# Layer 3's query-key and score products on 12-bit halves, in three passes

## The chip, the cores and the metric

The kernel runs on one core of one Trainium2 chip. The metric is the device time of one execution in microseconds. The kernel before has a median of 963.69 us over 3 runs (963.59 to 963.74). The profiled execution, from which all other times here are read, spans 961.7 us.

## The reference, cut to what matters

`x` is 32 graphs of 512 nodes with 128 features, `adj` one 512 x 512 matrix. Four layers follow each other, each of the form `x = x + layer(relu(layernorm(x)), adj)`. The change concerns the last one:

```python
def _L3_gnn_ref(x, A_shape, q, k, v):
    Q = x @ q
    K = x @ k
    A = jnp.einsum('bnd,bmd->bnm', Q, K)
    A = A / jnp.sqrt(jnp.float32(input_dimension))
    A = jnp.tanh(A / 8.0) * 8.0
    A = jnp.exp(A) * A_shape
    A = A / jnp.sum(A, axis=-1, keepdims=True)
    out = A @ x @ v
    return out
...
h = jnp.maximum(_layernorm(x, axis=-1), 0.0)
x = x + _L3_gnn_ref(h, adj, L3_gnn_q, L3_gnn_k, L3_gnn_v)
```

All of it is in 32-bit floating point.

## The kernel before, in words

A tile is 128 partitions by a free dimension. The 32 graphs are taken in 16 pairs, `q` = 0 to 15, with `b` = 0 or 1 inside a pair. `x` stays in SBUF from the first layer to the last. Layer 0 is recorded in an order written out by hand; from layer 1 on, each pair of a layer is a Python generator (`layer1(r)`, `layer2(q)`, `layer3(q)`), and the loop at the end of the kernel steps all active generators in turn and lets one new one in per turn. The Tile framework's scheduler then sets the order on each engine within the data dependences. Each engine works its own queue off in order.

One pair of layer 3 goes through these stages. `normed` makes `h` on ScalarE, `transposed` turns it to `hT` (features on partitions) with 32 x 32 transposes on VectorE (L283) and two trips through DRAM. Then for each `b`:

- **qkh** (L1097): one matmul of the constant `qk` = q k^T with `hT`, 128 x 512, into one PSUM bank; VectorE copies it to SBUF as `qkh` in another column order (L1100).
- **hv** (L435, called from L1102): `hT` times `vw`, four 128 x 128 matmuls; VectorE copies the result beside a column of ones (L1105).
- **scores** (L1110): four matmuls, each of a 128-column block of `hT` (stationary) with all of `qkh` (moving), 128 x 512, one PSUM bank each; ScalarE takes tanh out of PSUM (L1111), then exp in place (L1113); VectorE and GpSimd multiply by the transposed adjacency `adjTx` (L1115; odd blocks on GpSimd).
- **av** (L1125): 16 matmuls of 128 x 129 that weigh `hv` with `ex`; VectorE divides by the row sum and adds to `x` (L1127, L1130), and the result leaves by DMA (L1135).

The yields in `layer3` decide what stands between two stages of the same pair. In the middle of layer 3 the order on TensorE is, in every turn: av of one pair's second graph, scores of the next pair's second graph, av and then qkh and hv of younger pairs, scores of a younger pair's first graph, qkh and hv of the youngest.

All PSUM work shares 8 banks. In the program a 32-bit matmul is one instruction; the profile shows it as two MATMUL records, each with its own weight load (LDWEIGHTS).

Of the kernel before, what the change touches and what calls it, by code (L numbers as in the profile page):

```python
# [8 lines left out]

F32 = mybir.dt.float32  # L10
F16 = mybir.dt.float16
BF16 = mybir.dt.bfloat16
AF = mybir.ActivationFunctionType
OP = mybir.AluOpType
AX = mybir.AxisListType

P = 128
QR = 32
NQR = P // QR
NEG = 9000000000000000.0  # L20
EPS = 1e-5


@with_exitstack
def kernel(
# [37 lines left out]
    nc = tc.nc  # L63
    B, N, D = x.shape
# [5 lines left out]
    const = ctx.enter_context(tc.tile_pool(name="const", bufs=1))  # L70
# [3 lines left out]
    work = ctx.enter_context(tc.tile_pool(name="work", bufs=4))  # L74
    bounce = ctx.enter_context(tc.tile_pool(name="bounce", bufs=4, space=bass.MemoryType.DRAM))

    def bank(name):
        return psum.tile([P, 512], F32, tag="bank", name=name)

# [7 lines left out]
    def square_tile(name):  # L87
        return const.tile([P, NT, N], F32, tag="square", name=name, bufs=4)

    def crossed(ap):  # L90

        return ap.rearrange("p (a b c) -> p b a c", a=NT, b=NQR)

    def split(ap):
        return ap.rearrange("p (a b c) -> p a b c", a=NT, b=NQR)
# [13 lines left out]
    def x_tile(pool, bufs):  # L109

        x = pool.tile([P, 2, 2, NT, D], F32, tag="x", name=f"x_{len(xq)}", bufs=bufs)
        xq.append(x)
# [8 lines left out]
    def load_rows(ap, name):  # L121
        o = ap.shape[0] // P
        w = const.tile([P, o, ap.shape[1]], F32, name=name)
        nc.sync.dma_start(w, ap.rearrange("(o f) g -> f o g", f=P))
        return w

    def load_bcast(ap, name):
        w = const.tile([P, D], F32, name=name)
        nc.sync.dma_start(w, bass.AP(tensor=ap.tensor, offset=ap.offset, ap=[[0, P], [1, D]]))
        return w  # L130
# [7 lines left out]
    kw = load_rows(k_w, "kw")[:, 0, :]  # L138
    ecol = const.tile([P, NK], F32, name="ecol")
    nc.sync.dma_start(ecol, e_l0.rearrange("o (k p) -> p (o k)", p=P))  # L140
# [27 lines left out]
    by_source.__enter__()  # L168
    cols = prep.tile([P, N], F16, name="cols")
    nc.gpsimd.iota(cols, pattern=[[1, N]], base=0, channel_multiplier=0,  # L170
# [6 lines left out]
    eps = const.tile([P, 1], F32, name="eps")  # L177
    nc.vector.memset(eps, EPS)
    nc.scalar.activation(prep.tile([P, 1], F32, name="powers"), eps, AF.Exp)
# [4 lines left out]

    known = prep.tile([P, NT, 2], F16, name="known")
    nc.vector.tensor_copy(known[:, :, 1], rows)
    upto = prep.tile([P, NT, N], F16, name="upto")
    for t in range(NT):
# [3 lines left out]
    shift, scale = {}, {}  # L192
# [5 lines left out]
    def early_stats(q, whole):  # L198
# [7 lines left out]
        for b in range(2):  # L206
# [7 lines left out]
            half = slice(0 if whole else 2 * b, 2 * b + 2)  # L214
            nc.gpsimd.tensor_scalar(sd[:, half], st[:, half, :, 2], 1.0 / D, EPS, OP.mult, OP.add)
            nc.gpsimd.tensor_scalar(sh[:, half], st[:, half, :, 1], -1.0, None, OP.mult)
# [41 lines left out]
    def feature_major(name):  # L258
        return work.tile([P, NQR, 2, P], F32, tag="hT", name=name, bufs=4)
# [39 lines left out]
    sums = {}  # L299
# [65 lines left out]
    def products(name, form, left, right, evict, order=ORDER, on=lambda k, p: p):  # L365


        banks = {}
        for k, g, first in order:
            if first:  # L370
                banks[g] = bank(f"p_{name}_{g}")
            form(on(k, banks[g]), left[k], right[k], first)
            evict(k, banks[g])
            yield
# [18 lines left out]
    def mixed(name, left, right, dst):  # L393

        m1 = dst[:, 0, H:], dst[:, 1, :H], dst[:, 1, H:]

        def evict(k, p):
            p = p[:, :H]
            if k == 1:
                nc.scalar.copy(m1[0], p)  # L400
            elif k == 6:
                nc.vector.tensor_add(m1[1], p, m1[0])
            elif k == 7:
                nc.vector.tensor_add(m1[2], p, m1[0])
            elif k == 5:
                return
            elif k == 2:
                nc.scalar.copy(dst[:, 0, :H], p)
            elif k == 4:
                nc.vector.tensor_add(dst[:, 0, H:], p, m1[0])  # L410
            elif k == 3:
                nc.vector.tensor_add(dst[:, 1, :H], p, m1[1])

        def evict2(k, p):
            evict(k, p)
            if k == 5:
                held.append(p)
            if k == 7:
                nc.vector.tensor_add(dst[:, 1, H:], held[0][:, :H], m1[2])

        held = []
        return products(name, by_feature, left, right, evict2)

    def at(hT, b):
        return lambda t: hT[:, t, b, :]
# [75 lines left out]

    m = prep.tile([P, NT, N], F16, name="m")
    rc = prep.tile([P, NT], F32, name="rc")
    att = square_tile("att")
    ident16 = prep.tile([P, P], F16, name="ident16")
    nc.gpsimd.tensor_copy(ident16, ident)
    keep_busy(12)
    for t in range(NT):
        nc.vector.tensor_scalar(m[:, t, :], adj_s[:, t, :], 0.0, None, OP.is_gt, OP.add,
                                accum_out=rc[:, t : t + 1])  # L510
        nc.gpsimd.tensor_scalar(att[:, t, :], m[:, t, :], -1.0, -NEG, OP.add, OP.mult)
    rch = prep.tile([P, NT], F16, name="rch")
    nc.vector.tensor_copy(rch, rc)

    pi = bank("p_incl")
    for t in range(NT):
        for s in range(t + 1):
            nc.tensor.matmul(pi[:, t : t + 1], upto[:, s, blk(t)], rch[:, s : s + 1],
                             start=(s == 0), stop=(s == t))
# [12 lines left out]
    qk = const.tile([P, D], F32, name="qk")  # L532
# [16 lines left out]
    parts = []  # L549
    for i in range(3):  # L550
        eh = prep.tile([P, NK], BF16, name=f"eh_{i}")
        nc.gpsimd.tensor_copy(eh, ecoln)
        part = prep.tile([P, NK], F32, name=f"part_{i}")
# [5 lines left out]
    hT = {q: feature_major(f"hT0_{q}") for q in range(4)}  # L559
# [5 lines left out]
    for t in range(NT):  # L565
# [4 lines left out]
        for j in range(NT):  # L570
            nc.tensor.matmul(pg[j // 2][:, j % 2, :], m[:, t, blk(j)], of_row[:, t, :],
                             start=(t == 0 and j % 2 == 0), stop=(t == NT - 1), skip_group_check=True)
    pb = bank("p_known")[:, : 2 * NK].rearrange("p (k e) -> p k e", e=2)
    for kk in range(NK):
        for t in range(NT):
            nc.tensor.matmul(pb[:, kk, :], of_row[:, t, blk(kk)], known[:, t, :],
                             start=(t == 0), stop=(t == NT - 1))
# [17 lines left out]
    for kk in range(NK):  # L595
        for j in range(NT):
            nc.tensor.matmul(pw[kk][:, j * P :], pgs[:, j, blk(kk)], upto[:, j, j * P :],
                             start=(j == 0), stop=(j == NT - 1), skip_group_check=True)
# [100 lines left out]
    late = ctx.enter_context(tc.tile_pool(name="late", bufs=4))  # L699
# [341 lines left out]
        yield  # L1041
        ln_stats(NQ - 1)

    msgs, values = [], {}

    def values_tile(q, b):

# [41 lines left out]
    def layer3(q):  # L1089
        h = normed(q)  # L1090
        yield
        hT = transposed(h, f"hT3_{q}")
        yield
        yield
        for b in range(2):
            pp = bank(f"p_qkh_{q}_{b}")
            nc.tensor.matmul(pp, qk, hT[:, :, b, :], start=True, stop=True)  # L1097
            both = values_tile(q, b)
            qkh = both[:, :N]
            nc.vector.tensor_copy(crossed(qkh), split(pp))  # L1100

            pv = projected(f"p_hv_{q}_{b}", (at(hT, b), vw))  # L1102
            hv = both[:, N : N + NT * (D + 1)].rearrange("p (t f) -> p t f", f=D + 1)
            nc.vector.memset(hv[:, :, D : D + 1], 1.0)
            nc.vector.tensor_copy(hv[:, :, :D], pv)  # L1105
            yield
            ex = square_tile(f"ex_{q}_{b}")
            for t in range(NT):
                ps = bank(f"p_score_{q}_{b}_{t}")
                nc.tensor.matmul(ps, hT[:, t, b, :], qkh, start=True, stop=True)  # L1110
                nc.scalar.activation(ex[:, t, :], ps, AF.Tanh, scale=1.0 / (8.0 * math.sqrt(D)))  # L1111
            for t in range(NT):
                nc.scalar.activation(ex[:, t, :], ex[:, t, :], AF.Exp, scale=8.0)  # L1113
                eng = nc.gpsimd if t % 2 and q + b > 0 else nc.vector
                eng.tensor_mul(split(ex[:, t, :]), split(ex[:, t, :]), crossed(adjTx[0][:, t, :]))  # L1115
            yield
            out_r = out[2 * q + b].rearrange("(t p) f -> p t f", p=P)
            rsum = stats.tile([P, NT], F32, tag="rsum", name=f"rsum_{q}_{b}", bufs=4)
            final = b == 1 and q == NQ - 1
            n = 1 if final else 2  # L1120
            for i0 in range(0, NT, n):
                po = bank(f"p_av_{q}_{b}_{i0}").rearrange("p (i f) -> p i f", i=2)[:, :n]
                for i in range(n):
                    for t in range(NT):
                        nc.tensor.matmul(po[:, i, : D + 1], ex[:, t, blk(i0 + i)], hv[:, t, :],  # L1125
                                         start=(t == 0), stop=(t == NT - 1))
                nc.vector.reciprocal(rsum[:, i0 : i0 + n], po[:, :, D])  # L1127
                for i in range(n):
                    xi = xt[q][:, b, i0 + i, :]
                    nc.vector.scalar_tensor_tensor(xi, po[:, i, :D], rsum[:, i0 + i : i0 + i + 1], xi,  # L1130
                                                   OP.mult, OP.add)
                if final:
                    nc.sync.dma_start(out_r[:, i0, :], xt[q][:, b, i0, :])
            if not final:
                nc.sync.dma_start(out_r, xt[q][:, b])  # L1135
# [69 lines left out]
```

## Time and profile before

| | busy us | share of the span |
|---|---|---|
| TensorE matmuls (PE) | 953.3 | 99% |
| TensorE weight loads (PEld, overlap the matmuls) | 780.8 | 81% |
| VectorE (DVE) | 584.4 | 61% |
| ScalarE (ACT) | 469.1 | 49% |
| GpSimd (POOL) | 423.8 | 44% |

| group of layer 3 | records | busy us |
|---|---|---|
| p_av L1125, matmuls | 1024 | 119.9 |
| p_score L1110, matmuls | 256 | 115.2 |
| p_hv L435, matmuls | 256 | 33.7 |
| p_qkh L1097, matmuls | 64 | 32.7 |
| exp L1113, ScalarE | 128 | 76.7 |
| tanh L1111, ScalarE | 128 | 71.9 |
| mask L1115, GpSimd | 62 | 80.3 |
| mask L1115, VectorE | 66 | 46.1 |

A group's line gives the busy time of all its records together and the mean length of one. Matmul records overlap: [...]the mean length of one (593 ns for p_score) is more than the distance between two starts. What a matmul costs a busy TensorE is that distance, and the view of the chain of work that ended last, in order of time, gives it, since there each step counts only from the end of the step before. An average over the whole span says little here: the four layers have different loads, and the change touches only the last 300 us or so.

### The profile page before, as it was taken

To read this page: it belongs to the slowest core of one execution; us is meant where nothing else is said; L and a number is where in the kernel's file an instruction comes from. 1 tells how busy PE (TensorE), PEld (TensorE's weight loads), DVE (VectorE), ACT (ScalarE), POOL (GpSimd) and SP (SyncE) were. 2 spreads that over 40 slices of the span, in tenths; PEclk is the share of its full clock that TensorE was granted. 3 is DMA by queue.
4 is the path that set the end of the run, shared out by engine and by line. 5 is a ranking of instruction groups with operands and counts; after the bars stand their busy time and mean duration, and the time that the engine had idled before them with its cause. 6 is when DMAs were issued, how large, how long until landed. Compare 5 with 4: busy or idle time off the path is not lost.

```text
span 961.7 us, 15152 instructions
## 1 busy us (share of the span) xinstructions
PE 953.3 (99%) x5465; PEld 780.8 (81%) x5465; DVE 584.4 (61%) x1326; ACT 469.1 (49%) x1054; POOL 423.8 (44%) x470
## 2 busy tenths in 40 slices
PE   8999999999999999999999999999999999999998
PEld 4899999898989999899877777777677777767776
DVE  8888885846536545656667665665654444444444
ACT  5865542442232233277627655444765445544553
POOL 5878987833517522513333444433032233223322
PEclk9999999999999999999999999999999999999999
DMA  9356532441341230343333433223121121211111
GB/s 252 62 166 185 160 108 84 104 110 55 102 136 45 66 88 23 110 110 96 89 99 97 126 91 85 74 82 88 56 88 56 55 77 44 72 61 45 55 33 44
DMA packets 83913, 86.04 MB, mean 89 GB/s; under 512 B 6784, under 2 KB 74624, under 8 KB 83840
## 3 DMA queue, kind: packets, MB, share of 16 engines
q1 hardware_dynamic: 83552, 84.57, 31.6%
q8 instruction: 43, 0.70, 0.3%
q10 hardware_dynamic: 288, 0.52, 0.2%
q14 instruction: 30, 0.25, 0.1%
HBM read 44.17 MB, written 40.89 MB: 88 GB/s over the span
## 4 chain that ended last, share of the span: by engine, by line
PE 96%; ACT 2%; DVE 1%; DMA 0%; POOL 0%; issue 0%; DVEq 0%; ACTq 0%
PE p_av L1125 12%; PE p_score L1110 11%; PE p_l_c L386 8%; PE p_w L435 6%; PE p_l_d L386 6%; PE p_msgT_c L379 5%; PE p_l_a L386 4%; PE p_x1T_c L379 4%; PE p_l L435 3%; PE p_feat L435 3%; PE p_hv L435 3%; PE p_qkh L1097 3%; PE p_x1T_a L379 3%; PE p_msgT_d L379 3%; PE p_g L435 3%; PE p_x1T_d L379 3%
## 5 line engine op out<-in xcount | busy, mean ns | idle before, releaser
L247 ACT ACTIVATE h<-x,sh,rs 128x128 f32<-128x128 f32 x512 | 209.2, 484 | 51.7 <-PE p_x1T_d L379 21.7
L1115 POOL TENSOR_TENSOR ex<-ex,adjTx 128x512 f32<-128x512 f32 x62 | 80.3, 1295 | 208.3 <-ACT ex L1113 202.8
L1111 ACT ACTIVATE ex<-p_score 128x512 f32<-128x512 f32 x128 | 71.9, 587 | 122.8 <-issue 113.0
L1125 PEld LDWEIGHTS p_av<-qkh_hv,ex 128*128 128x128 f32 x1024 | 118.4, 191 | 8.4 <-issue 7.4
L1125 PE MATMUL p_av<-qkh_hv,ex 128*128 128x129 f32 x1024 | 119.9, 274 | 0.0
L1110 PE MATMUL p_score<-qkh_hv,hT 128*128 128x512 f32 x256 | 115.2, 593 | 0.0
L283 DVE STREAM_TRANSPOSE hb_hT<-h 128x512 f32<-128x512 f32 x120 | 82.0, 698 | 23.7 <-ACT h L247 22.6
L1115 DVE TENSOR_TENSOR ex<-ex,adjTx 128x512 f32<-128x512 f32 x66 | 46.1, 703 | 82.0 <-ACT ex L1113 81.9
L227 DVE BATCH_NORM_STATS2 bn<-x 128x6 f32<-128x256 f32 x248 | 89.8, 419 | 0.6
L1110 PEld LDWEIGHTS p_score<-qkh_hv,hT 128*128 128x128 f32 x256 | 46.2, 190 | 46.5 <-issue 44.5
L1113 ACT ACTIVATE ex<-ex 128x512 f32<-128x512 f32 x128 | 76.7, 630 | 1.9
L356 POOL TENSOR_TENSOR rt_feat<-feat,feat 128x256 f32<-128x256 f32 x16 | 11.6, 725 | 136.4 <-ACT feat L1064 136.4
L958 ACT COPY w<-p_w 128x512 f32<-128x512 f32 x32 | 18.2, 574 | 106.1 <-PE p_w L435 106.1
L356 POOL TENSOR_TENSOR rt_w<-w,rt_w 128x512 f32<-128x512 f32 x16 | 20.4, 1273 | 110.3 <-DVE rt_w L356 92.0
L435 PE MATMUL p_w<-th,x1T 128*128 128x128 f32 x256 | 49.5, 275 | 0.0
L435 PE MATMUL p_w<-th,hs 128*128 128x128 f32 x256 | 49.5, 275 | 0.0
L435 PEld LDWEIGHTS p_hv<-vw,hT 128*128 128x128 f32 x256 | 33.6, 192 | 15.3 <-issue 8.1
L1075 POOL TENSOR_TENSOR x<-x,phi2b 128x256 f32<-128x256 f32 x64 | 44.5, 727 | 0.0
L435 PEld LDWEIGHTS p_w<-th,hs 128*128 128x128 f32 x256 | 39.9, 192 | 0.7
L1064 ACT ACTIVATE feat<-feat 128x512 f32<-128x512 f32 x32 | 20.1, 629 | 41.4 <-DVE feat L1063 41.4
L1130 DVE SCALAR_TENSOR_TENSOR x<-p_av,rsum,x 128x128 f32<-128x128 f32 x128 | 39.1, 347 | 1.9
L712 POOL TENSOR_TENSOR hd<-hT,adiag 128x512 f32<-128x512 f32 x32 | 39.6, 1274 | 0.2 <-ACT adiag L838 0.2
(238 smaller groups left out, 2039.7 us busy)
## 6 DMA issues: line engine op xcount, KB each, us to landing
d_hT<-hb_hT SPq DMA_DIRECT2D x240, 128.0 KB
hT<-d_hT SPq DMA_DIRECT2D x60, 512.0 KB
x<-in_x_dram SPq DMA_DIRECT2D x32, 256.0 KB
out_dram<-x SPq DMA_DIRECT2D x31, 256.0 KB
adjT_d<-adj_squares SPq DMA_DIRECT2D x4, 256.0 KB
sq<-in_adj_dram SPq DMA_DIRECT2D x4, 256.0 KB
adjTx<-adjT_d SPq DMA_DIRECT2D x4, 256.0 KB
adj_s<-in_adj_dram ACTq DMA_DIRECT2D x2, 256.0 KB
```

Of the source, the lines that this page charges most:

```text
L227: nc.vector.bn_stats(st[:, k].rearrange("p e s -> p (e s)"), xt[q][:, b, t : t + 2, :].rearrange("p t f -> p f t"))
L247: nc.scalar.activation(h[:, b, t, :], xt[q][:, b, t, :], AF.Relu, bias=shift[q][:, i : i + 1], scale=scale[q][:, i : i + 1])
L283: nc.vector.transpose(hb[:, :, b].rearrange("p j t r -> p t j r"), h[:, b].rearrange("p t (j c) -> p t j c", c=QR))
L379: nc.tensor.matmul(p[:, :H], b[:, k, :], a[:, k, :], start=(first and k == 0), stop=(k == 1), skip_group_check=True)
L386: nc.tensor.matmul(p[:, i * 2 * D : (i + 1) * 2 * D], a[:, k, blk(i)], b[:, k], start=(first and i == 0 and k == 0), stop=(k == 1), skip_g ...
L435: nc.tensor.matmul(p[:, blk(t)], hT(t), w, start=(i == 0), stop=(i == len(terms) - 1))
L1075: tc.keep_in_program_order(nc.gpsimd.tensor_add(xi, xi, spread(phi2b, 2)))
L1110: nc.tensor.matmul(ps, hT[:, t, b, :], qkh, start=True, stop=True)
L1111: nc.scalar.activation(ex[:, t, :], ps, AF.Tanh, scale=1.0 / (8.0 * math.sqrt(D)))
L1113: nc.scalar.activation(ex[:, t, :], ex[:, t, :], AF.Exp, scale=8.0)
L1115: eng.tensor_mul(split(ex[:, t, :]), split(ex[:, t, :]), crossed(adjTx[0][:, t, :]))
L1125: nc.tensor.matmul(po[:, i, : D + 1], ex[:, t, blk(i0 + i)], hv[:, t, :], start=(t == 0), stop=(t == NT - 1))
```

## The change

A 32-bit operand is split into two halves of 12 bits. A product of two split operands has four partial products; the change gets by with three. With e = 1/4096, H and L the halves of a moving operand x (x = H + L), H' the upper half of the other one, y, and L' = 4096 (y - H'), it forms M = x / (1 + e) - H and M' = H' - L'. Then

```
(1 + e) (H H' + L L' + M M') = x y
```

so three matmuls that add up in one PSUM bank give x y / (1 + e), and the factor 1 + e goes into the scale of the operation that reads the bank. Each half is written in the type `float32r`, whose matmul TensorE takes as it is, in place of a full 32-bit product.

Per pair and graph, `moving_parts` makes three key tiles from `hT` (one ScalarE copy, one GpSimd subtraction, one VectorE operation), which serve both qkh and scores. The copy of qkh out of PSUM becomes a multiplication by 4097 (L1142 of the new file), and `scaled_parts` makes three query tiles from it, one after the other on ScalarE, VectorE and GpSimd. `fixed_parts` splits the constant `qk` once. The key tiles of the first graph are made one yield ahead of qkh, those of the second right after the scores of the first. They are put into buffers that earlier layers use (tags "hs", "u", "rt", "sums"). hv and av stay as they were.

```diff
+    def moving_parts(x, high, low, mid):
+
+        nc.scalar.activation(high, x, AF.Copy, scale=DOWN)
+        nc.gpsimd.tensor_sub(low, x, high.bitcast(F32))
+        nc.vector.scalar_tensor_tensor(mid, x, 1.0 / UP, high.bitcast(F32), OP.mult, OP.subtract)
+
+    def scaled_parts(x_low, high, low, mid):
+
+        nc.scalar.activation(high, x_low, AF.Copy, scale=DOWN / LOW)
+        nc.vector.scalar_tensor_tensor(low, high.bitcast(F32), -LOW, x_low, OP.mult, OP.add)
+        nc.gpsimd.tensor_sub(mid, high.bitcast(F32), low.bitcast(F32))
...
@@ -1091,13 +1120,28 @@
         yield
         hT = transposed(h, f"hT3_{q}")
         yield
+        keys = {}
+
+        def key_parts(b):
+            keys[b] = [late.tile([P, NQR, P], F32R, tag="hs", name=f"key_{part}_{q}_{b}", bufs=6) for part in PARTS[:2]]
+            keys[b].append(work.tile([P, NQR, P], F32R, tag="u", name=f"key_{PARTS[2]}_{q}_{b}", bufs=3))
+            moving_parts(hT[:, :, b, :], *keys[b])
+
+        if not qk_parts:
+            parts = const.tile([P, 3, D], F32R, tag="sums", name="qk_parts", bufs=2)
+            qk_parts.extend(parts[:, i, :] for i in range(3))
+            fixed_parts(qk, *qk_parts)
+        key_parts(0)
         yield
         for b in range(2):
             pp = bank(f"p_qkh_{q}_{b}")
-            nc.tensor.matmul(pp, qk, hT[:, :, b, :], start=True, stop=True)
+            for i in range(3):
+                nc.tensor.matmul(pp, qk_parts[i], keys[b][i], start=(i == 0), stop=(i == 2))
             both = values_tile(q, b)
             qkh = both[:, :N]
-            nc.vector.tensor_copy(crossed(qkh), split(pp))
+            nc.vector.tensor_scalar(crossed(qkh), split(pp), UP * LOW, None, OP.mult)
+            query = [work.tile([P, N], F32R, tag="rt", name=f"query_{part}_{q}_{b}", bufs=6) for part in PARTS]
+            scaled_parts(qkh, *query)
...
             for t in range(NT):
                 ps = bank(f"p_score_{q}_{b}_{t}")
-                nc.tensor.matmul(ps, hT[:, t, b, :], qkh, start=True, stop=True)
-                nc.scalar.activation(ex[:, t, :], ps, AF.Tanh, scale=1.0 / (8.0 * math.sqrt(D)))
+                for i in range(3):
+                    nc.tensor.matmul(ps, keys[b][i][:, t, :], query[i], start=(i == 0), stop=(i == 2))
+                nc.scalar.activation(ex[:, t, :], ps, AF.Tanh, scale=UP / (8.0 * math.sqrt(D)))
+            if b == 0:
+                key_parts(1)
```

`fixed_parts` splits `qk` in the same way with two ScalarE copies and two GpSimd subtractions on 128 x 128.

More of the change, by code (lines that the diff above doesn't have):

```diff
@@ L10 @@
 F32 = mybir.dt.float32
+F32R = mybir.dt.float32r
 F16 = mybir.dt.float16
@@ L20 @@
 NEG = 9000000000000000.0
+PARTS = ("high", "low", "mid")
 EPS = 1e-5
+LOW = 4096.0
+DOWN = 1.0 - 1.0 / 8192.0
+UP = 1.0 + 1.0 / 4096.0
 @with_exitstack
@@ L422, in mixed, with fixed_parts @@
         return products(name, by_feature, left, right, evict2)
+    def moving_parts(x, high, low, mid):
[6 more added lines that the diff above has]
+        nc.gpsimd.tensor_sub(mid, high.bitcast(F32), low.bitcast(F32))
+    def fixed_parts(x, high, low, mid):
+        nc.scalar.activation(high, x, AF.Copy, scale=DOWN)
+        nc.gpsimd.tensor_sub(x, x, high.bitcast(F32))
+        nc.scalar.activation(low, x, AF.Copy, scale=LOW)
+        nc.gpsimd.tensor_sub(mid, high.bitcast(F32), low.bitcast(F32))
     def at(hT, b):
@@ L1042, in layer1_stats @@
         ln_stats(NQ - 1)
-    msgs, values = [], {}
+    msgs, values, qk_parts = [], {}, []
     def values_tile(q, b):
```

## Prediction

> **What bounds the kernel now.** I read the page's first two parts, then the chain of waits, then that chain in order of time inside layer 3, then the busy times of one turn of layer 3.
>
> ```profile
> PE 953.3 (99%) x5465; PEld 780.8 (81%) x5465; DVE 584.4 (61%) x1326; ACT 469.1 (49%) x1054; POOL 423.8 (44%) x470
> PE   8999999999999999999999999999999999999998
> PEclk9999999999999999999999999999999999999999
> ```
>
> TensorE is busy in every slice at the full granted clock, the last 300 us included. The chain that ended last says the same by line:
>
> ```profile
> PE 96%; ACT 2%; DVE 1%; DMA 0%; POOL 0%; issue 0%; DVEq 0%; ACTq 0%
> PE p_av L1125 12%; PE p_score L1110 11%; PE p_l_c L386 8%; PE p_w L435 6%; PE p_l_d L386 6%; PE p_msgT_c L379 5%; PE p_l_a L386 4%; PE p_x1T_c L379 4%; PE p_l L435 3%; PE p_feat L435 3%; PE p_hv L435 3%; PE p_qkh L1097 3%; PE p_x1T_a L379 3%; PE p_msgT_d L379 3%; PE p_g L435 3%; PE p_x1T_d L379 3%
> ```
>
> The lines that change, p_score and p_qkh, are 14% of the chain. One whole turn of layer 3 (one pair of graphs) in order of time; columns are start, length, step:
>
> ```profile
> 804.02 3.58 PE p_av L1125 x32
> 807.61 0.86 PE p_qkh L1097 x2
> 808.47 0.89 PE p_hv L435 x8
> 809.36 3.44 PE p_score L1110 x8
> 812.79 0.86 PE p_qkh L1097 x2
> 813.65 0.89 PE p_hv L435 x8
> 814.54 3.58 PE p_av L1125 x32
> 818.12 3.43 PE p_score L1110 x8
> ```
>
> It is 17.53 us of TensorE and nothing else: no wait between the steps. So in layer 3 a us less on TensorE is a us less in the end, as long as the others keep up. Their load in a window of one turn (PE, PEld, DVE, ACT, POOL):
>
> ```profile
> 808.30:825.82 17.52, 17.52 (x101) 12.73 (x100) 8.41 (x23) 8.70 (x16) 5.13 (x4) 1.00 0.20 61
> ```
>
> No engine but TensorE is over half full. (The layernorm of layer 3 has been done before: the window holds no such record.)
>
> **What the Trainium skill says.** "FP8 and Floating Point Precision", section "TensorE Precision Notes": true 32-bit takes four passes through the array, and a reduced-precision 32-bit form reads the four bytes and cuts them. The trace agrees on the four: eight score records, four products, take 3.44 us, 0.86 each. One pass of 512 columns is seen early in the trace, where six bf16 matmuls of 128x512 run from 20.00 to 21.29, 0.215 each, a quarter of 0.86:
>
> ```profile
> 20.00 1.46 PE L635 MATMUL p_val<-at_part,at_row 128*128 128x512 bf16 x6
> 21.29 0.59 PE L631 MATMUL p_later<-at_col,at_row 128*128 128x512 bf16 x2
> ```
>
> No run yet shows a float32r matmul. "TensorE: Matmul & The Clock Gate", section "LDWEIGHTS (loading the stationary operand)": 128 columns of weights in 128/1.2 = 107 ns. The trace agrees: p_hv's eight records, each with its own 32-bit load, take 0.89 us, 0.111 each, so a load fits under a pass of 0.215.
>
> **The change part by part.**
>
> *Removed and added on TensorE.* Per turn, 2 qkh and 8 score products: 10 x 0.859 = 8.59 us (the four rows 0.86, 3.44, 0.86, 3.43). New: 10 products x 3 matmuls. Cost of one, from both sides: 0.215 us if it is one pass, 0.43 if it takes two, 0.859 if it is run as full 32-bit. I take one pass: the old records already stream four-byte operands at 0.215 per pass, so the width of the operand doesn't slow a pass, and the page asks for four passes only for true 32-bit. Then 30 x 0.215 = 6.45 us, saving 2.14 per turn; the turn is 15.39. Over 16 turns: **34.3 us**. Weight loads go from 2 to 3 per product; each hides under the pass before it (0.111 under 0.215).
>
> *Added on the other engines*, all 128x512, priced by the nearest rows (mean ns of one):
>
> ```profile
> L1115 POOL TENSOR_TENSOR ex<-ex,adjTx 128x512 f32<-128x512 f32 x62 | 80.3, 1295 | 208.3 <-ACT ex L1113 202.8 <-DVE ex L1115 5.5
> L1113 ACT ACTIVATE ex<-ex 128x512 f32<-128x512 f32 x128 | 76.7, 630 | 1.9
> L1115 DVE TENSOR_TENSOR ex<-ex,adjTx 128x512 f32<-128x512 f32 x66 | 46.1, 703 | 82.0 <-ACT ex L1113 81.9
> ```
>
> Per turn 4 ScalarE copies, 4 VectorE operations, 4 GpSimd subtractions. ScalarE 8.70 + 4 x 0.60 = 11.1 us; VectorE 8.41 + 4 x 0.70 = 11.2; GpSimd 5.13 + 4 x 1.30 = 10.3. All stay under the new 15.39, at 67 to 73%. The multiplied copy of qkh reads the same bank as the old one (0.69 us): nothing. Unknown is whether GpSimd pays for writing float32r: 1.30 from the row, twice that, 2.6, as the upper end (a second pass over the tile); I take 1.30.
>
> *The new wait.* Scores now wait for copy (0.69), ScalarE (0.60), VectorE (0.70), GpSimd (1.30) in series, 3.3 us and some 0.5 for hand-overs, where they waited for the copy alone. In the middle of layer 3 this is covered. From the qkh of a second graph to its scores stand hv 0.89, scores 2.58, qkh and hv 1.54, av 3.58 = 8.6 us; from that of a first graph hv, av, scores, av, qkh, hv = 12.2 us. The order of the changed program puts the query copy on ScalarE behind the exps of the scores before it: I laid one turn out by hand with these durations. ScalarE is through its eight operations and a key copy about 6 us after the scores began, then waits for the copy out of PSUM, then the tanh of the next scores; the query tiles of a second graph are ready about 5 us before TensorE wants them, those of a first graph about 6. Behind the waiting copy stand only tanhs whose scores aren't done yet. The key tiles are made half a turn ahead, and their buffers come free as the scores of an older graph end, where ScalarE has just arrived. PSUM banks: each is read out 5 us or more before its next use. So the steady turns lose nothing.
>
> *Where it isn't covered.* At the **end**, between the last qkh and its scores stand only hv:
>
> ```profile
> 946.89 0.89 PE p_hv L435 x8
> 947.78 3.65 PE p_score L1110 x8
> 951.44 7.16 PE p_av L1125 x64
> ```
>
> Before, the copy fits under hv to 0.2 us. After, counted from the start of that qkh: bank full at 0.82, VectorE still adding the last av until 1.1, copy until 1.8, upper query half at 2.45 against TensorE free at 1.54: 0.9 lost. The order has the four upper passes first (to 3.3), two lower ones (to 3.7), then waits for GpSimd until 4.6: 0.9 more. The scores then end close together, so tanhs and exps (8 x 0.55) and GpSimd's second mask end near 10.9, when av of the graph before (3.58) has ended at 9.5: about 0.9 more past the first av passes. Sum 2.6 us. At the **start** of layer 3, 677 to 700 us, ScalarE is nearly full: layernorms of the last pairs, and table loads of 1.28 us for tanh against square root, in the trace at 679.1, 686.5 and 689.6. The changed order puts the query copy of pair 0's second graph behind two of these loads; laid out, it comes 1.4 us late, its GpSimd part 0.6, and the av that follows waits some 1.5 for masks queued behind the new GpSimd work. 3.5 us, bounds 0 and 8. `fixed_parts` (128x128, once) is queued long before layer 3 and costs nothing.
>
> Sum: 963.7 - 34.3 + 2.6 + 3.5 = **935.5 us**.
>
> **The rivals.**
> (1) *GpSimd or ScalarE becomes the bound.* If a GpSimd write in float32r takes 2.6 us, its turn is 5.13 + 10.4 = 15.5 against 15.39, with masks and query parts waiting for each other; an estimated 0.8 us per turn more, 13 in all: **948**. For it: no trace shows this write. Against: the subtraction is the operation of the row, on the same bytes.
> (2) *A float32r matmul isn't one pass.* With two, a product is 6 passes where it was 4: 160 products x 2 x 0.215 = 69 us more, 963.7 + 69 + 4 = **1037**, slower; at full price far more. For it: nothing in the trace has this type. Against: the page's reduced form, and the four-byte streams at 0.215.
> (3) *The waits at both ends are absorbed*, since the scheduler reordered those stretches: 963.7 - 34.3 = **929.4**, the floor.
>
> **How the numbers follow.** Forecast 0.77, (1) 0.10, (2) 0.08, (3) 0.05. The forecast's own spread is 930 to 943 (start 0 to 8, tail 1 to 4, a us or two from steady turns). Low end 929, the floor; the high end 946 takes in part of (1); outside stay (2) and the rest of (1), under 0.2. Faster by over 0.2%: 0.91; slower: 0.08; within: 0.01, as no case ends near 963.
>
> **What would show it.** Right: p_score passes 0.215 us apart and 2.58 per graph in the chain; a turn of 15.4 us; TensorE still over 95% of the chain; two short gaps, near the first scores and the last. Wrong: score starts 0.43 or more apart (rival 2); GpSimd subtractions near 2.6 us and query parts ahead of TensorE's waits in each turn (rival 1); loads that no longer hide, shown as starts between 0.215 and 0.43; or ScalarE waits growing over the turns, which would mean that my hand-laid turn missed a buffer.

## The result and the profile after

The changed kernel takes **946.29 us** (median of 4 runs, 946.18 to 947.55), the kernel before 963.64 beside it: a ratio of **0.9823, 95% interval 0.9809 to 0.9837**. That is 17.35 us saved where 28.2 were forecast. The profiled executions span 961.7 us before and 944.4 after.

Busy times and the 40 slices on the page of the changed kernel (each digit is tenths of a slice):

```profile
PE 929.0 (98%) x5625; PEld 811.2 (86%) x5625; DVE 685.4 (73%) x1390; ACT 499.1 (53%) x1120; POOL 543.8 (58%) x536
PE   8999999999999999999999999999989999999997
DVE  8888885745555545556667766565699999999995
POOL 5878997933428524421624334433467878787873
PEclk9999999999999999999999999999999999999999
```

TensorE is still busy everywhere. What is new stands in the DVE row: from slice 30 on (685 us, some 20 us before the steady turns of layer 3 begin) VectorE is at 9 in every slice but the last. An average of 73% hides that. (The page's chain of waits holds next to nothing for this kernel, so I read layer 3 from the order of time.)

One turn of TensorE after the change; columns are start, length of the record, step (records overlap, so a length is more than the distance to the next start):

```profile
807.10 3.74 PE L1172 MATMUL p_av<-qkh_hv,ex 128*128 128x129 f32 x32
810.60 0.47 PE L1155 MATMUL p_score<-query_high,key_high 128*128 128x512 f32 x1
810.91 0.39 PE L1155 MATMUL p_score<-query_low,key_low 128*128 128x512 f32 x1
811.14 0.40 PE L1155 MATMUL p_score<-query_mid,key_mid 128*128 128x512 f32 x1
811.37 0.40 PE L1155 MATMUL p_score<-query_high,key_high 128*128 128x512 f32 x1
811.61 0.39 PE L1155 MATMUL p_score<-query_low,key_low 128*128 128x512 f32 x1
...
813.45 3.78 PE L1172 MATMUL p_av<-qkh_hv,ex 128*128 128x129 f32 x32
816.98 0.48 PE L1139 MATMUL p_qkh<-key_high,qk_parts 128*128 128x512 f32 x1
```

Read the starts, not the lengths. A score pass starts 0.23 us after the one before it (0.230 at the median of 278 distances between 720 and 905 us); only the second after an av starts 0.31 after the first (twelve passes with this change of type from 810.60 to 813.45, 2.85 us). So a float32r matmul is a single pass, but not one of 0.215. The 0.31 is no loss of its own: the av before it takes 3.50 us from its start to the next step (807.10 to 810.60), where it took 3.58. The busy times of the turn that ends there (PE, PEld, DVE, ACT, POOL):

```profile
801.10:816.98 15.88, 15.88 (x113) 14.62 (x112) 15.15 (x27) 10.56 (x20) 12.80 (x9) 1.00 0.21 68
```

The turn is 15.88 us and TensorE full in it, as forecast; VectorE has 15.15 where 11.2 were forecast, GpSimd 12.80 where 10.3 were, ScalarE 10.56 where 11.1 were. The groups of operations show which grew (the last columns: busy, mean ns of one):

```profile
L1162 POOL TENSOR_TENSOR ex<-ex,adjTx 128x512 f32<-128x512 f32 x62 | 105.0, 1713 | 6.7 <-issue 5.7 <-ACT ex L1160 1.1
L1162 DVE TENSOR_TENSOR ex<-ex,adjTx 128x512 f32<-128x512 f32 x66 | 87.5, 1331 | 18.4 <-ACT ex L1160 18.4
L437 POOL TENSOR_TENSOR key_low<-hT,key_high 128x512 fp32r<-128x512 f32 x32 | 54.5, 1702 | 32.2 <-ACT key_high L436 29.7 <-PE p_msgT_d L384 2.5
L444 POOL TENSOR_TENSOR query_mid<-query_high,query_low 128x512 fp32r<-128x512 f32 x32 | 41.2, 1288 | 41.5 <-PE p_qkh L1139 22.2 <-DVE query_low L443 19.3
```

The masks, which the change doesn't touch, went from 703 to 1331 ns on VectorE and from 1295 to 1713 on GpSimd. Writing float32r costs GpSimd nothing: query_mid takes 1288. In order of time the cause is plain. VectorE (start, length):

```profile
805.60 0.69 DVE L443 SCALAR_TENSOR_TENSOR query_low<-query_high,qkh_hv 128x512 fp32r<-128x512 f32 x1 [0.16 <-ACT query_high L442]
...
808.78 0.68 DVE L438 SCALAR_TENSOR_TENSOR key_mid<-hT,key_high 128x512 fp32r<-128x512 f32 x1
...
809.98 1.17 DVE L1162 TENSOR_TENSOR ex<-ex,adjTx 128x512 f32<-128x512 f32 x1
811.07 1.78 DVE L443 SCALAR_TENSOR_TENSOR query_low<-query_high,qkh_hv 128x512 fp32r<-128x512 f32 x1
```

and GpSimd in the same stretch:

```profile
802.67 1.74 POOL L1162 TENSOR_TENSOR ex<-ex,adjTx 128x512 f32<-128x512 f32 x1
806.43 1.27 POOL L444 TENSOR_TENSOR query_mid<-query_high,query_low 128x512 fp32r<-128x512 f32 x1 [2.02 <-PE p_qkh L1139]
808.76 1.83 POOL L437 TENSOR_TENSOR key_low<-hT,key_high 128x512 fp32r<-128x512 f32 x1 [1.06 <-ACT key_high L436]
810.56 3.44 POOL L1162 TENSOR_TENSOR ex<-ex,adjTx 128x512 f32<-128x512 f32 x2
```

The same operation takes 0.69 us while GpSimd rests, and 1.78 while GpSimd is in two masks: 1.1 us more, close to one GpSimd operation. The two engines take turns. VectorE's key_mid ends at 809.46, and GpSimd's key_low, which began with it, 1.13 us later; the VectorE mask that began before that end ends 0.56 us after it. It is so at every meeting: read record by record from 720 to 905 us, 68 VectorE operations on two tiles that began while GpSimd was at work ended 0.55 us after GpSimd's, and 68 GpSimd operations the other way round ended 1.13 to 1.16 us after VectorE's. The time that an engine stands still is inside the length of its record and shows as busy, not as a wait. The Trainium skill has this in "SBUF — State Buffer", section "Who interferes with whom": "A DVE instruction with two SBUF inputs contends with a GpSimd instruction that reads SBUF", and it calls the contention an exclusive lock. The trace agrees. VectorE's copies out of PSUM, which have one input, stay at 0.68 throughout.

Where the time went, in stretches of layer 3 read from the starts of TensorE's steps: *start* from the first qkh to the first of the fourth pair; *middle* from there to the last qkh, 12.9 turns; *tail* from the last qkh to the last matmul. The forecast column is the prediction's own terms sorted into them (2.14 saved per turn; 5 products of the last graph in the tail; 3.5 and 2.6 lost).

| us | before | forecast | after | upper halves alone (e1) | the same in bf16 (e2) |
|---|---|---|---|---|---|
| start | 49.44 | 47.3 | 49.45 | 46.37 | 45.72 |
| middle | 226.04 | 198.4 | 206.11 | 204.44 | 198.77 |
| tail | 12.72 | 14.3 | 14.74 | 13.26 | 13.14 |
| sum | 288.20 | 260.0 | 270.30 | 264.07 | 257.63 |

The first qkh of the changed kernel also comes 0.6 us later (670.98 against 670.39). 17.9 less 0.6 is the 17.3 us by which the spans differ.

### The profile page after: what moved, and what is told of

It reads as the page before. It is cut to its first block, busy times and chain, and to the rows that moved or that the text cites. A ratio compares the mean times of both kernels' runs of the same rounds, so it can differ in the third digit from the quotient of the medians.

```text
span 944.4 us, 15678 instructions
## 1 busy us (share of the span) xinstructions
PE 929.0 (98%) x5625; PEld 811.2 (86%) x5625; DVE 685.4 (73%) x1390; ACT 499.1 (53%) x1120; POOL 543.8 (58%) x536
## 5 line engine op out<-in xcount | busy, mean ns | idle before, releaser
L1162 POOL TENSOR_TENSOR ex<-ex,adjTx 128x512 f32<-128x512 f32 x62 | 105.0, 1713 | 6.7 <-issue 5.7
L1162 DVE TENSOR_TENSOR ex<-ex,adjTx 128x512 f32<-128x512 f32 x66 | 87.5, 1331 | 18.4 <-ACT ex L1160 18.4
L1156 ACT ACTIVATE ex<-p_score 128x512 f32<-128x512 f32 x128 | 69.7, 591 | 17.7 <-PE p_score L1155 17.6
L1160 ACT ACTIVATE ex<-ex 128x512 f32<-128x512 f32 x128 | 73.2, 638 | 0.8
L437 POOL TENSOR_TENSOR key_low<-hT,key_high 128x512 fp32r<-128x512 f32 x32 | 54.5, 1702 | 32.2 <-ACT key_high L436 29.7
L444 POOL TENSOR_TENSOR query_mid<-query_high,query_low 128x512 fp32r<-128x512 f32 x32 | 41.2, 1288 | 41.5 <-PE p_qkh L1139 22.2
L442 ACT ACTIVATE query_high<-qkh_hv 128x512 fp32r<-128x512 f32 x32 | 20.2, 633 | 65.0 <-DVE qkh_hv L1142 64.2
L1155 PE MATMUL p_score<-query_high,key_high 128*128 128x512 f32 x128 | 52.4, 417 | 1.9 <-ACT query_high L442 1.9
L1155 PE MATMUL p_score<-query_mid,key_mid 128*128 128x512 f32 x128 | 50.2, 396 | 0.8 <-POOL query_mid L444 0.8
L1155 PE MATMUL p_score<-query_low,key_low 128*128 128x512 f32 x128 | 49.4, 390 | 0.0
```

The source lines that it names most:

```text
L437: nc.gpsimd.tensor_sub(low, x, high.bitcast(F32))
L444: nc.gpsimd.tensor_sub(mid, high.bitcast(F32), low.bitcast(F32))
L1155: nc.tensor.matmul(ps, keys[b][i][:, t, :], query[i], start=(i == 0), stop=(i == 2))
L1156: nc.scalar.activation(ex[:, t, :], ps, AF.Tanh, scale=UP / (8.0 * math.sqrt(D)))
```

## Experiments

Theory A: TensorE's own pace, about 0.23 us a pass instead of 0.215, is the shortfall. Rival B: VectorE and GpSimd, which slow each other, are.

**e1: upper halves alone.** All three passes use the upper halves; the others aren't made (leaves out the precision of the lower halves).

```diff
-        nc.gpsimd.tensor_sub(low, x, high.bitcast(F32))
-        nc.vector.scalar_tensor_tensor(mid, x, 1.0 / UP, high.bitcast(F32), OP.mult, OP.subtract)
...
-            keys[b] = [late.tile([P, NQR, P], F32R, tag="hs", name=f"key_{part}_{q}_{b}", bufs=6) for part in PARTS[:2]]
+            keys[b] = [late.tile([P, NQR, P], F32R, tag="hs", name=f"key_high_{q}_{b}", bufs=6)] * 3
```

> Leaves out the lower and middle halves: all three passes of a product use the upper halves, so the results lose precision; four operations less per turn on VectorE and four on GpSimd. Theory A (TensorE's own pace: a float32r pass takes 0.229 us instead of 0.215): the turn stays at 15.9 us, float32r starts 0.229 apart, and only the two ends get shorter, in all about 941 us (939 to 944). Rival B (VectorE and GpSimd get in each other's way and pace the turns): the turn falls to 15.4 us and the whole to about 933 us (930 to 936).

Measured: 939.43 us (939.27 to 939.77), ratio 0.9746 (0.9732 to 0.9761). The turn is 15.85: without any of the added two-input work it is as long as with it. So the steady turn of the changed kernel is TensorE's. But the total is 6.9 us lower (6.6 by the spans of the profiles): 3.1 in the start, 1.5 in the tail, 0.4 ahead of the first qkh, and 1.7 in the middle, where the changed kernel has one av that starts 1.24 us late behind masks (0.96 of it at 734.61).

**e2: the same in bf16.** The edit of e1 with the upper halves as BF16 tiles.

> As the run with the upper halves alone, with these halves in bf16 (precision lost). If the longer pass belongs to the 4-byte type (its stream or its weight load): starts 0.215 apart, turn 15.4 to 15.5 us, some 7 us under the run with float32r upper halves. If it belongs to the place (three passes into one bank, one weight load per pass): starts stay at 0.229 and the time is the same as that run within 1 us.

Measured: 933.17 (932.88 to 934.67), ratio 0.968 (0.9663 to 0.9696); the turn is 15.41. One graph's scores in its trace:

```profile
811.58 2.75 PE L1149 MATMUL p_score<-query_high,key_high 128*128 128x512 bf16 x11
814.17 0.81 PE L1133 MATMUL p_qkh<-key_high,qk_parts 128*128 128x512 bf16 x3
```

From 811.58 to 814.17 are 2.59 us for twelve passes, 0.216 each (one record is missing), against 2.85 in the changed kernel. These passes, too, have each a weight load of their own and add up by threes in one bank, so the longer pass belongs to the type and not to its place. The middle, 198.77, is close to the forecast's 198.4. The type alone makes 6.4 us of layer 3.

**e3: twice as many passes of half the width.** e1 with each score pass cut in two of 256 columns.

```diff
-                    nc.tensor.matmul(ps, keys[b][i][:, t, :], query[i], start=(i == 0), stop=(i == 2))
+                    for c in range(2):
+                        nc.tensor.matmul(ps[:, c * 256 : c * 256 + 256], keys[b][i][:, t, :],
+                                         query[i][:, c * 256 : c * 256 + 256], start=(i == 0 and c == 0),
+                                         stop=(i == 2), skip_group_check=True)
```

> As the run with the upper halves alone, each score pass cut into two of 256 columns, each with its own weight load. If a fixed 0.014 us comes with each pass: starts 0.107 + 0.014 = 0.121 apart, 24 score passes per turn cost 0.31 us more, about 5 us in all over that run. If the stream itself is 6.5% slower: starts 0.1145 apart and no change (within 1 us). If a 4-byte weight load can't come more often than every 0.229 us: starts 0.229, 5.5 us more per turn, 88 us in all.

Measured: 941.56 (941.22 to 941.67), ratio 0.9767 (0.9753 to 0.9782); the turn is 16.06. 24 half passes take 2.95 us (starts 806.26 to 809.21), twelve whole ones in e1 2.86 (805.73 to 808.59): twelve more matmuls cost 0.09 us, 0.008 each. Over e1 the run takes 2.1 us more, between the 5 of a fixed 0.014 us per pass and the nothing of a slower stream, so it decides for neither. Nor does it tell a cost per matmul from one of the weight load: its score loads follow each other without idle time (0.0 us before them from 720 to 900 us, 9.4 in e1). What it rules out is a load that comes only every 0.229 us: these come some 0.12 apart.

**e4: the added work alone.** All halves are made; the products are done in full 32 bit as before.

```diff
-            for i in range(3):
-                nc.tensor.matmul(pp, qk_parts[i], keys[b][i], start=(i == 0), stop=(i == 2))
+            nc.tensor.matmul(pp, qk, hT[:, :, b, :], start=True, stop=True)
...
-                for i in range(3):
-                    nc.tensor.matmul(ps, keys[b][i][:, t, :], query[i], start=(i == 0), stop=(i == 2))
+                nc.tensor.matmul(ps, hT[:, t, b, :], qkh, start=True, stop=True)
```

> The halves are made as in the changed kernel, but qkh and scores are computed in full 32-bit from the unsplit tiles, as before: the added work alone. Theory A: TensorE still sets the turn at 17.5 us, no wait for halves: 964 to 967 us, the few us from the crowded start of layer 3. Rival B (the halves' work blocks what TensorE needs): the turn grows beyond 17.5 us and the time goes over 970 us. VectorE's and GpSimd's two-operand operations should be longer than before (0.70 and 1.29 us) in either case where they overlap.

Measured: 967.01 (966.71 to 968.29), ratio 1.0033 (1.002 to 1.0046). The turn stays 17.52, the middle 226.05, the tail 12.71: with TensorE at its old pace the added work costs only around the start, 3.1 us in all. (The start is 53.81 instead of 49.44, but 1.7 of the difference is a change of order: two groups of layer 2's products, 0.86 us each, stand behind the first qkh here.) The waits of TensorE there:

```profile
668.03 1.13 PE L384 MATMUL p_msgT_c<-sq,rt_feat 128*128 128x256 f32 x4 [0.41 <-DVE msgT L407]
672.25 1.10 PE L384 MATMUL p_msgT_c<-sq,rt_feat 128*128 128x256 f32 x4 [1.37 <-DVE msgT L409]
673.83 1.13 PE L384 MATMUL p_msgT_d<-sums_sq,feat 128*128 128x256 f32 x4 [0.48 <-DVE msgT L424]
```

These are products of layer 2, whose results VectorE takes out of PSUM. And VectorE stood idle 1.26 us for an upper key half of ScalarE, with the next of these results behind it in its queue:

```profile
670.69 1.08 DVE L438 SCALAR_TENSOR_TENSOR key_mid<-hT,key_high 128x512 fp32r<-128x512 f32 x1 [1.26 <-ACT key_high L436]
671.69 0.41 DVE L409 TENSOR_TENSOR msgT<-p_msgT_c,msgT 128x256 f32<-128x256 f32 x1
```

**e5: no product of the two lower halves.** Upper by upper, upper by lower, lower by upper: the middle halves fall away, two operations each on VectorE and GpSimd per turn (leaves out only the product of the lower halves).

```diff
+PAIRS = ((0, 0), (1, 0), (0, 1))
...
-        nc.vector.scalar_tensor_tensor(mid, x, 1.0 / UP, high.bitcast(F32), OP.mult, OP.subtract)
...
+                for i, (s, m) in enumerate(PAIRS):
+                    nc.tensor.matmul(ps, keys[b][s][:, t, :], query[m], start=(i == 0), stop=(i == 2))
```

> The three passes are upper*upper + upper*lower + lower*upper; only the product of the two lower halves is left out. The middle halves are no longer made: per turn two VectorE operations and two GpSimd operations fewer than in the changed kernel, the same 30 float32r passes on TensorE. Theory A (TensorE's own pace sets the turn, the added VectorE and GpSimd work costs only at both ends of layer 3): a turn of 15.85 to 15.9 us as in the changed kernel (15.88) and in the run with upper halves alone (15.85), and a total between theirs, 939.4 and 946.3, near 941, since half of the added work is gone and no query part waits for GpSimd. Rival B (the shared load of VectorE and GpSimd paces the turns): a shorter turn, below 15.7, and a total below 939.

Measured: 941.93 (941.85 to 942.03), ratio 0.9773 (0.9759 to 0.9788). Turn 15.86, start 47.55, tail 13.56: between e1 and the changed kernel in each stretch, as theory A had it.

**e6: all the work on halves, but bf16 passes.** The halves are made with the changed kernel's instructions, and TensorE reads the upper ones in bf16 (leaves out the precision of the lower halves). As the upper half is bf16 here, the other halves are made from the unsplit tile in its place, so they don't wait for ScalarE.

```diff
-                    nc.tensor.matmul(ps, keys[b][i][:, t, :], query[i], start=(i == 0), stop=(i == 2))
+                    nc.tensor.matmul(ps, keys[b][0][:, t, :], query[0], start=(i == 0), stop=(i == 2))
```

> All halves are made with the instructions of the changed kernel, but TensorE reads only the upper ones, in bf16, three times (leaves out the precision of the lower halves). TensorE's turn alone is 15.41 us, as in the run with bf16 upper halves. It asks whether VectorE and GpSimd only slow each other while both read two tiles, or exclude each other. If they exclude each other over the whole length of an operation, the two-input work of one turn adds up to 8 x 0.69 on VectorE and 8 x 1.27 on GpSimd, 15.7 us, and the turn is 15.7 or longer, the total above 944. If the operations are only stretched in part, the turn stays at 15.4 and the total is 933.2 plus what both ends of layer 3 cost in the changed kernel, 6.9 us, so 940.

Measured: 943.86 (943.72 to 945.15), ratio 0.9797 (0.9781 to 0.9814). The first four steady turns are 15.41, then they take 15.7 to 16.9 until the last one or two, about 16.3 at the median. The total is close to the 944 of the first case, not to 940. Sixty microseconds of the long ones:

```profile
780.00:840.00 60.00, 59.07 (x401) 43.91 (x407) 56.15 (x99) 36.68 (x71) 41.59 (x30) 1.00 0.23 71
```

VectorE is 94% busy and TensorE no longer full; most of its listed waits are for masks (0.34 us each at 811.35, 860.53 and 877.01). TensorE has the same passes as in e2, which keeps 15.41 to the end, so the long turns come from the added VectorE and GpSimd work. That they begin only after four turns looks like a lead that is used up; this was not shown. **So rival B lies just below A**: by this run, a TensorE at 0.215 a pass would not have kept its turn of 15.39 beside this work.

**e7: no square roots at the start.** e5, with the inverse roots of the last two layernorms of layer 2 on GpSimd, so that ScalarE needs no table for them.

```diff
+            nc.gpsimd.tensor_scalar(sd, st[:, :, :, 2], 1.0 / D, EPS, OP.mult, OP.add)
+            nc.gpsimd.tensor_tensor(rs, sd, minus_half, OP.pow)
...
-        ln_stats(q)
+        ln_stats(q, q >= NQ - 2)
```

> As the run that drops the product of the lower halves, and the last two layernorms of layer 2 take their inverse root on GpSimd (a power of -1/2) instead of ScalarE's square root, so that two table loads of 1.28 us leave ScalarE at the start of layer 3. If ScalarE's table loads hold up the first query halves, 1 to 1.5 us less than that run. If the start is held by VectorE and GpSimd, no change or up to 1 us more, since GpSimd gets two more operations there. The steady turn stays at 15.85 to 15.9 under both.

Measured: 942.90 (942.49 to 944.60), ratio 0.9787 (0.9772 to 0.9801), and a start of 49.69 against 47.55 in e5. The run gains nothing, but it doesn't clear the table loads. The wait for a query half went from 1.36 us in e5 (at 696.04, for a lower half of VectorE) to 0.15. In exchange GpSimd's power takes 1.67 us, the layernorm behind it comes later, the first tanhs of layer 3 begin at 682.19 instead of 679.88, and an av waits 1.37 us for a mask of VectorE.

**e8: both ends in full 32 bit.** e7, and the first two graphs and the last one take their products whole.

```diff
+            whole = (q, b) in ((0, 0), (0, 1), (NQ - 1, 1))
+            if whole:
+                nc.tensor.matmul(pp, qk, hT[:, :, b, :], start=True, stop=True)
```

> As the run before it, and the first two graphs and the last one of layer 3 take their query-key and score products in full 32 bit, so that nothing on TensorE waits for a query half at either end. It costs 3 x 5 x (0.86 - 0.69) = 2.6 us of TensorE, and by theory A gives back the tail (1.5 us, what the last scores waited for VectorE and GpSimd) and the waits of the first scores and first av (about 3 us): some 2 us less than the run before it, near 938. If the first stretch is held by the masks of VectorE and GpSimd in any case, 0 to 1.5 us more than the run before it.

Measured: 942.21 (941.81 to 942.89), ratio 0.9777 (0.9763 to 0.9792). The tail fell from 13.56 to 12.81 though the last graph's products cost 0.86 more; the start (49.04) kept a wait of 0.88 for a mask. No gain over e5, and not the 938 of theory A.

**e9: the GpSimd subtractions on VectorE.** The same exact products as the changed kernel.

```diff
-        nc.gpsimd.tensor_sub(low, x, high.bitcast(F32))
+        nc.vector.tensor_sub(low, x, high.bitcast(F32))
...
-        nc.gpsimd.tensor_sub(mid, high.bitcast(F32), low.bitcast(F32))
+        nc.vector.tensor_sub(mid, high.bitcast(F32), low.bitcast(F32))
```

> The changed kernel with the four GpSimd subtractions of a turn moved to VectorE; the same exact products. If a two-input VectorE operation and a GpSimd operation exclude each other, this shortens what they need together in a turn from 8 x 0.69 + 8 x 1.27 = 15.7 us to 12 x 0.69 + 4 x 1.27 = 13.4, though VectorE gets more work: the turn stays 15.88 (TensorE), the waits for masks at the start of layer 3 and for query halves at its end shrink, and the total is 940 to 942. If VectorE is simply full and GpSimd's share relieved it, the masks come later than in the changed kernel and the total is 946 or more.

Measured: 949.93 (949.65 to 952.77), ratio 0.9863 (0.9848 to 0.9878): slower than the changed kernel, and my theory of the moment, that only the sum of both engines' locked time counts, fell. One turn:

```profile
801.51:817.90 16.39, 16.10 (x113) 14.62 (x112) 15.68 (x31) 10.46 (x20) 6.47 (x5) 1.00 0.22 66
```

VectorE has 8.41 + 8 x 0.69 = 13.9 us of its own here, and 1.8 of waiting for GpSimd's four masks; it is at 96% of a turn of 16.39, and TensorE waits for masks. What counts here is VectorE's queue: its own work plus what it stands still for GpSimd. The sum of the locked time was also set too high: of each operation only the 0.55 and 1.13 us seen above shut the other engine out, so the changed kernel's eight and eight of a turn need an estimated 13.4 us, not 15.7.

**e10: the same move in e6** (bf16 passes, leaves out the precision of the lower halves).

> The run with bf16 upper halves and all the work on halves (943.9, ten turns of about 16.4 us), with its GpSimd subtractions moved to VectorE (leaves out the precision of the lower halves). If the two engines exclude each other, every steady turn is 15.41 us and the total 935 to 938. If VectorE's own load is the limit (8.4 + 8 x 0.7 = 14 us if nothing stretches it), the turns stay near 16.4 and the total at 943 or more.

Measured: 942.29 (941.44 to 942.47), ratio 0.9775 (0.9761 to 0.979). Turns between 15.41 and 17.1, mean 16.0. Both sides missed: not 15.41 in every turn, not 16.4 either. VectorE is full:

```profile
780.00:840.00 60.00, 58.77 (x424) 46.45 (x423) 59.24 (x119) 38.51 (x74) 21.31 (x14) 1.00 0.23 71
```

**e11: the same move in e5.**

> The run that leaves out the product of the two lower halves (941.9), with the two GpSimd subtractions of a turn moved to VectorE: turn 15.85; if the exclusion costs at both ends, 939 to 940.5, near the run with upper halves alone (939.4); if not, 941.9 or more.

Measured: 941.87 (941.49 to 942.22), ratio 0.9772 (0.9758 to 0.9787): no difference from e5. With the middle halves gone VectorE has room either way (49.40 of 60 us, 45.24 in e5).

**e12: three bf16 passes.** e11 with bf16 halves, upper and rest, so that some 16 bits of each operand are kept (leaves out the rest and the product of the lower halves).

```diff
-        nc.scalar.activation(high, x, AF.Copy, scale=DOWN)
-        nc.gpsimd.tensor_sub(low, x, high.bitcast(F32))
+        nc.scalar.copy(high, x)
+        nc.vector.tensor_sub(low, x, high)
```

> As the run before it, but the halves are bf16 (upper: rounded to bf16; lower: the rest rounded to bf16), so a product keeps some 16 bits instead of 23: three bf16 passes at 0.215 us. Theory A: a turn of 15.41, 16 x 0.45 = 7 us less than the run before it, 932 to 934, the fastest that keeps more than the upper halves. If VectorE and GpSimd become the bound at this pace, turns above 15.6 and a total above 936.

Measured: **934.70** (934.54 to 935.22), ratio 0.9699 (0.9683 to 0.9715), 7.2 us below e11 where 7 were expected from the pace; every steady turn is 15.41. It beats both kernels, at the price of precision; e5, which drops only the smallest product, is 4.4 us faster than the changed kernel.

## Why the prediction was wrong in size

The direction held, and TensorE's own work as the bound; 10.9 of the 28.2 us were missing. Two steps failed. The first is the price of a float32r pass, "I take one pass" at 0.215 us: it measured 0.230, so a turn saves 1.675 us (17.525 less 15.85, e1) and 16 turns 26.8, not 34.3. That is 7.5 of the 10.9. The second is "All stay under the new 15.39, at 67 to 73%": VectorE and GpSimd keep each other waiting, and VectorE came to 15.15 us a turn. The other 3.4 us are a stall of 1.7 in the middle, which e1 doesn't have, and some 1.8 more at the start, ahead of it and in the tail than was forecast. By the prediction's steps:

- **The bound, and the saving per turn.** TensorE alone set the turn, as read, and a float32r matmul is one pass. The turn is a sum: 8.94 us for av and hv as before, and 30 passes, which at 0.230 make 15.84 (e1: 15.85) and at bf16's 0.216 make 15.42 (e2: 15.41). The reason given for 0.215, that the old records stream four-byte operands at it, spoke of the passes of a full 32-bit matmul; they don't price a float32r one. The middle gave 19.9 us instead of 27.6; of the 7.7 missing, the type explains 5.7 (e1 against e2) and the stall 1.7. The two bounds were 0.215 and 0.43; nothing in between was worked out, though the prediction's last part named it ("loads that no longer hide, shown as starts between 0.215 and 0.43"). That a load hides was read from 0.111 us, which is the distance of p_hv's matmuls; the load records last 192 ns there, 188 for the float32r scores and 98 for bf16 (e2). Whether the load makes the 0.014 us stays open.
- **The load of the other engines.** ScalarE was right (10.56). VectorE was forecast at 11.2 and came to 15.15, GpSimd at 10.3 and came to 12.80, because durations were taken from rows of a kernel in which the two seldom met. The section "Who interferes with whom", quoted above, was not used. VectorE's 11.2 plus 4.0 of standing still is the 15.15.
- **"So the steady turns lose nothing"** was all but true: 15.88 with the added work, 15.85 without (e1), and one stall of 1.24 us. It was true by a small margin that the prediction did not know of, as e6 shows, and so in part by luck.
- **The start, 3.5 us.** The three waits foreseen came in the places named: the query half (1.4 forecast), its GpSimd part (0.6), the av behind its masks (1.5):

```profile
695.32 1.20 PE L1155 MATMUL p_score<-query_high,key_high 128*128 128x512 f32 x4 [1.06 <-ACT query_high L442]
...
697.48 0.98 PE L1155 MATMUL p_score<-query_mid,key_mid 128*128 128x512 f32 x3 [0.28 <-POOL query_mid L444]
...
699.83 0.46 PE L1172 MATMUL p_av<-qkh_hv,ex 128*128 128x129 f32 x2 [0.90 <-DVE ex L1162]
700.86 0.94 PE L1172 MATMUL p_av<-qkh_hv,ex 128*128 128x129 f32 x6 [0.57 <-POOL ex L1162]
```

  That is 2.8 us. With the steps around them stretched as well, hv, scores, av, qkh and hv take 12.96 us from 693.21 to 706.17, where a steady turn needs 8.7 for them: 4.2 lost for the 3.5 forecast. The cause named for the first wait is there too. VectorE's copy out of PSUM was done at 692.48, but the query copy on ScalarE stood behind a square root and a tanh, each with its table load:

```profile
691.24 1.28 ACT L238 ACT_TABLE_LOAD   x1
692.54 0.30 ACT L238 ACTIVATE sd<-bn,eps 128x8 f32<-128x8 f32 x1
692.86 1.28 ACT L1156 ACT_TABLE_LOAD   x1
694.15 0.60 ACT L1156 ACTIVATE ex<-p_score 128x512 f32<-128x512 f32 x1
694.65 0.62 ACT L442 ACTIVATE query_high<-qkh_hv 128x512 fp32r<-128x512 f32 x1
```

  The loads alone don't make the wait: e1 has the same two, at 688.21 and 689.83, and waits for no query half there. Beside the added halves they come 3 us later. No run takes them out of the changed kernel (e7 starts from e5). So this term was nearly right, in place and in size. The stretch saved nothing (49.45 against 49.44) because its 26 products gave 4.4 us at the measured pace, not 5.6. e1 loses 1.1 us between the same steps, so the added halves cost 3.1 of the 4.2. Not foreseen were 0.4 us ahead of the first qkh (after against e1), where layer 2's last products are stretched.
- **The tail, 2.6 us**, measured 2.9 (14.74 against 12.72, with 5 products of 0.17 us saving each): upper half 0.82 late, GpSimd's half 0.49, av behind a mask 0.63; the rest is spread over the steps around them.

```profile
929.19 1.20 PE L1155 MATMUL p_score<-query_high,key_high 128*128 128x512 f32 x4 [0.82 <-ACT query_high L442]
...
931.35 0.73 PE L1155 MATMUL p_score<-query_mid,key_mid 128*128 128x512 f32 x2 [0.49 <-POOL query_mid L444]
...
938.11 3.17 PE L1172 MATMUL p_av<-qkh_hv,ex 128*128 128x129 f32 x26 [0.63 <-POOL ex L1162]
```

- **The rivals.** (2), two passes, is out. (1) came close in its number, 948, by luck: GpSimd writes float32r at its usual 1.29 us, and it was VectorE that filled. (3), no loss at the ends, is out.

Together, in layer 3: 257.63 us with bf16 and only the upper halves made (e2), 6.4 for the type (e1), 6.2 for the other halves (after) make the 270.30; the forecast had 260.0, so it allowed 2.4 for what cost 12.7.

Open: what in the type makes a float32r pass 0.014 us longer than a bf16 one; and why e6's turns, once they are long, are longer (16.3) than the changed kernel's 15.88 with nearly the same work; the order in which the two engines meet differs, and that was not taken apart.

## What to carry to other kernels

Before adding VectorE and GpSimd work that reads two tiles from SBUF, look at both together: a duration from a trace in which the engines seldom meet is a lower bound, and each meeting here cost VectorE up to 1.1 us. Look for one shape with two durations; these waits show as busy time. When TensorE is relieved, look at the next engine's busy time in the changed stretch, not in the whole span; here VectorE came within 5% of the new turn. Moving GpSimd's share to VectorE doesn't help where VectorE's queue is nearly full (e9). The passes of a full 32-bit matmul don't tell what a matmul of another type costs; where the type is new to the trace, carry a value between the bounds.

## What the runs showed of the hardware

- A float32r matmul of 128x512 with its own load starts 0.23 us after the last, a bf16 one 0.216, a full 32-bit one takes 0.86; cut into 256 columns, float32r takes 0.123 (e3). The second float32r matmul after a full 32-bit one starts 0.31 after the first, and the 32-bit group before it is shorter by about the 0.08 us that this is more.
- VectorE operations on two tiles and GpSimd operations on two tiles, all 128x512, exclude each other: where they met, VectorE's ended 0.55 us after GpSimd's, GpSimd's 1.13 to 1.16 after VectorE's. Alone they take 0.69 and 1.27 us; in the steady turns of the changed kernel they take up to 1.78 and 1.84.
- VectorE's copies out of PSUM stay at 0.68 us beside GpSimd.
- A GpSimd subtraction that writes float32r costs the same as a multiplication that writes plain 32 bit (1.29 against 1.30 us); a ScalarE copy into it takes 0.63.
